# Packed attention scores, id transfers issued by ScalarE, and other part sizes in a graph-attention kernel

## The chip, the core and the metric

The kernel runs on one core of a Trainium2 chip. The core has five engines, each with its own instruction queue that it works through in order: PE (TensorE, matrix products into PSUM; PEld is its loading of stationary operands), DVE (VectorE), ACT (ScalarE), POOL (GpSimd) and SP (SyncE, which here only issues transfers). Transfers run on 16 DMA engines; SP, ACT and POOL can issue them. The metric is the device time of the kernel in microseconds.

## What is computed

One graph-attention layer with residual and two norms, over 12500 nodes and 412500 edges (D = 128, 64 edge features, 8 heads):

```python
h, q, k, v = (x @ W + b for each of Wn, Wq, Wk, Wv)
eh = edge_features @ We + be
hmid   = leaky_relu(concat(q[src], k[tgt], eh) @ A1 + b1, 0.2)
scores = leaky_relu(hmid @ A2 + b2, 0.2)            # 8 heads
w      = softmax(scores.mean(axis=-1), axis=0)      # over all edges
out    = segment_sum(w[:, None] * v[tgt], src)
y      = layernorm(h + out) * gamma + beta
return layernorm(x + y)
```

## The kernel before

Nodes lie in 98 blocks of 128, edges in 403 groups of 1024. The edges come in order of their target node; the sum goes by source node. So the kernel works in two halves.

**Making** (`make(p)`). For each group of a part p it builds one-hot matrices of the targets on DVE (lines 836 to 857), multiplies them on PE with the group's rows of the key and value table (line 914), adds the edge features' product (line 919), copies the result from PSUM to a record tile `rec` on ACT (lines 929 and 930), and POOL scatters the records by source block into a table in DRAM (line 941, eight scatters a group). Stage 0 makes part 0 alone, with the tables of the nodes and further index work spread between its groups.

**Summing** (`sums_of`). A part's table holds for each block a fixed number of tiles of 128 records, `plan.tiles[p]`, enough for the mean number of its edges and 4.4 standard deviations; unused places are masked. A unit is two blocks: 10, 12 or 14 tiles with 5, 6 or 7 tiles a block, 49 units a part. For each unit:

- SP loads the records `rt` (line 1109) and the blocks' query rows `qs`.
- `sources` makes the masked ids `sl` on DVE, `turn` transposes them on PE (line 1139), `turned` turns them into bytes `slT` on DVE (line 1146), `put` stores them in DRAM (`row`, line 1153) and `spread` loads them back, repeated over all partitions (`rowB`, line 1158). SP issues both transfers, and the second waits until the first has landed.
- For each piece of up to four tiles: one-hot `ohT` on DVE (line 1170), hidden layer on PE (lines 1184 and 1193), and its leaky rectifier in two steps, ACT (line 1204) and DVE (line 1208).
- `scores`: four products with `A2s` as the stationary operand, each over a fourth of the unit's tiles, into four strips of 32 PSUM partitions (line 1221). The 32 columns of `A2s` hold the eight heads and two columns of their sum, scaled, from which the linear part of the leaky rectifier comes. `above_zero` applies Relu with the bias on ACT (line 1235), and `heads` sums over heads: a product with `headsum` for each of three or four tile positions (line 1247).
- `maxima`, `maximum`, `reference` lower the running maximum over all partitions (lines 1257 to 1277), `weights` takes the exponential (line 1286), `select` and `weigh` make the weighted one-hots `ohw` (lines 1295 and 1309), and `add` sums the values by node (line 1338). `total` joins the partial sums of earlier parts (line 1354).

Stage p (1 to 5) interleaves the making of part p with the summing of part p - 1; then part 5 is summed alone, and the closing applies the softmax's sum and the norms. The parts are cut by `CUTS`, in groups; the last part ends at 403.

What sets the order: the engines' instructions stand in the order in which the program is written, with no reordering. A unit's operations are placed at steps by the offsets of `lags` and `last_lags` (eight steps from one unit to the next, six in the last part), and the steps are spread evenly over the six steps of each group being made. A line on an fp32 product stands for two passes on PE, so line 1221 has eight passes a unit. A record in the profile is one pass.

PSUM has eight banks: two for `pkv`, one for the counts, two for `ph`, one for `psc` (shared by the transposed ids and the scores) and two for `psm`.

## Time and profile before

| | us |
|---|---|
| median of three runs (4974.44 to 4991.73) | 4985.54 |
| the profiled execution | 4977.97 |
| its span | 4976.3 |

| engine | busy us | share of the span |
|---|---|---|
| PE | 4076.9 | 82% |
| PEld | 3176.9 | 64% |
| DVE | 4181.3 | 84% |
| ACT | 3168.0 | 64% |
| POOL | 3327.3 | 67% |

The granted clock of TensorE is 0.93 over the span, and the DMA engines move 294 GB/s. The busy shares are means over stages whose loads differ: making alone, making and summing together with different numbers of tiles a group, summing alone. They say little by themselves, so the span is best read in stretches, cut where a part ends (the mask of a part, line 978, is built once its last group is counted). Issuing a transfer and waiting for a semaphore are not counted as busy. An engine's wait is put down to whatever came last.

### The profile page before, as it was taken

The page shows a single profiled execution, that of the slowest core. Times are in us where ns is not written, and L with a number is a line of the kernel's source. Part 1 is how long each engine was busy: PE and PEld are TensorE (multiplying, and loading weights), DVE is VectorE, ACT ScalarE, POOL GpSimd, SP SyncE. Part 2 cuts the span into 40 slices and gives each one's busy share as a digit, 9 for nine tenths or more (in the row PEclk, how much of TensorE's full clock was granted, in tenths as well). Part 3 has the DMA queues.
Part 4 walks back from the last instruction along what each step waited for, and adds up shares of the span by engine and source line. Part 5 has one row for each costly group of instructions (what it writes and reads, how often), then busy time and mean ns, then how long its engine had stood idle before and what let it go on. Part 6 is the DMA issues. An engine that isn't in the chain of part 4 may idle for free. (4 is left out here: it accounts for less than half of the span.)

```text
span 4976.3 us, 87101 instructions
## 1 busy us (share of the span) xinstructions
PE 4076.9 (82%) x27267; PEld 3176.9 (64%) x27568; DVE 4181.3 (84%) x9010; ACT 3168.0 (64%) x8326; POOL 3327.3 (67%) x3280
## 2 busy tenths in 40 slices
PE   3665547878888989988988888988889888889997
PEld 2444435666666766776766676776667666666786
DVE  7888867888888888888988887888889898877777
ACT  2442224655656777777777776777777666667785
POOL 3777777777777777777777777767667777731003
PEclk7787868999999999999999999999999999999999
DMA  5888978999888998888898888888888898889864
GB/s 187 285 288 272 369 246 300 317 318 307 275 280 295 315 310 308 311 307 299 315 308 310 303 310 280 306 303 307 297 297 302 300 312 304 298 289 308 302 238 171
DMA packets 603263, 1462.23 MB, mean 294 GB/s; under 512 B 103678, under 2 KB 329105, under 8 KB 600996
## 3 DMA queue, kind: packets, MB, share of 16 engines
q1 hardware_dynamic: 447696, 1027.15, 62.9%
q0 software_dynamic: 154752, 429.39, 22.7%
q8 instruction: 220, 3.60, 0.3%
q14 instruction: 255, 2.09, 0.1%
q10 hardware_dynamic: 340, 0.01, 0.0%
HBM read 884.13 MB, written 585.06 MB: 295 GB/s over the span
## 5 line engine op out<-in xcount | busy, mean ns | idle before, releaser
L941 POOL DMA_INDIRECT rtab<-rec,idx x3224 | 3242.7, 1006 | 1150.6 <-issue 783.3
L929 ACT ACTIVATE rec<-pkv 128x1024 f32<-128x1024 f32 x806 | 821.6, 1019 | 1162.7 <-PE pkv L919 519.1
L1309 ACT ACTIVATE ohw<-ohs,w 128x128 f32<-128x128 bf16 x3822 | 1256.1, 399 | 121.8 <-DVE ohs L1295 59.0
L1338 PE MATMUL psm<-rt,ohw 128*128 128x128 f32 x7644 | 1085.4, 285 | 3.4 <-ACT ohw L1309 0.8
L1338 PEld LDWEIGHTS psm<-rt,ohw 128*128 128x128 f32 x7644 | 997.7, 197 | 101.4 <-ACT hm L1204 13.0
L919 PE MATMUL pkv<-WeS,eat 128*128 128x256 f32 x3224 | 920.5, 412 | 0.0
L1208 DVE TENSOR_TENSOR hm<-ph,hm 128x512 f32<-128x512 f32 (+1 forms) x1029 | 662.5, 644 | 265.9 <-ACT hm L1204 261.2
L914 PE MATMUL pkv<-kvs,ohd 128*128 128x256 bf16 x3224 | 530.0, 291 | 290.5 <-ACT rec L929 283.0
L1184 PE MATMUL ph<-ident,rt 128*128 128x128 f32 x3822 | 625.4, 284 | 118.1 <-DVE hm L1208 112.9
L1170 DVE TENSOR_SCALAR ohT<-rowB,iotaP,power 128x512 bf16<-128x512 uint8 (+2 forms) x1176 | 598.0, 519 | 93.0 <-DMA rowB<-row 92.7
L914 PEld LDWEIGHTS <-ohd 128*128 128x128 bf16 x3224 | 317.0, 103 | 540.6 <-issue 423.4
L919 PEld LDWEIGHTS pkv<-WeS,eat 128*128 128x128 f32 x3224 | 606.4, 209 | 70.2
L1184 PEld LDWEIGHTS ph<-ident,rt 128*128 128x128 f32 x3822 | 442.2, 146 | 323.9 <-issue 144.9
L1204 ACT ACTIVATE hm<-ph 128x512 f32<-128x512 f32 (+1 forms) x1029 | 567.0, 551 | 33.8 <-PE ph L1193 26.8
L857 DVE TENSOR_SCALAR ohd<-dstb,node 128x1152 bf16<-128x1152 uint8 x404 | 564.9, 1398 | 0.0
L1193 PE MATMUL ph<-ohT,qs 128*128 128x512 bf16 (+2 forms) x2051 | 531.6, 340 | 29.2 <-DVE ohT L1170 14.5
L883 DVE TENSOR_TENSOR ats<-pc,oh 128x792 f32<-128x792 f32 x403 | 391.1, 970 | 37.1 <-PE pc L865 37.1
L1221 PE MATMUL psc<-hm,A2s 128*32 128x384 f32 (+2 forms) x2352 | 360.0, 550 | 63.1 <-DVE hm L1208 34.4
L1295 DVE TENSOR_TENSOR ohs<-iotaE,sl 128x512 bf16<-128x512 bf16 (+1 forms) x1029 | 409.1, 398 | 1.0 <-ACT ohw L1309 1.0
L847 DVE TENSOR_REDUCE few<-oh 128x99 bf16<-128x792 bf16 x403 | 395.1, 980 | 13.9
L894 DVE TENSOR_REDUCE pos<-ats 128x8 f32<-128x792 f32 x403 | 389.1, 966 | 1.7
L1247 PE MATMUL psm<-headsum,z 128*128 128x4 f32 (+1 forms) x2058 | 256.7, 245 | 58.0 <-DVE part L1354 50.8
(192 smaller groups left out, 3876.2 us busy)
## 6 DMA issues: line engine op xcount, KB each, us to landing
rt<-rtab SPq DMA_DIRECT2D x147, 1820.0 KB
rt<-rtab SPq DMA_DIRECT2D x147, 1560.0 KB
eat<-in_ea SPq DMA_DIRECT2D x201, 512.0 KB
rtab<-rec,idx POOLq DMA_INDIRECT x3224
dstb<-dtab SPq DMA_DIRECT2D x201, 256.0 KB
rtab<-empty SPq DMA_DIRECT2D x76, 520.0 KB
qs<-qtab SPq DMA_DIRECT2D x294, 128.0 KB
atab<-part SPq DMA_DIRECT2D x294, 128.0 KB
```

Source lines behind the costliest of these rows:

```text
L857: nc.vector.tensor_scalar(to, ids[:, cols], node, None, op0=ALU.is_equal)
L914: nc.tensor.matmul(pk[:, i, h, :], ohd[t], kvs, start=(h == 0), stop=False,)
L919: nc.tensor.matmul(pk[:, i, :, :D], eat[:, (j + i) * P : (j + i + 1) * P], WeS, start=False, stop=True,)
L929: nc.scalar.activation(rec[:, :, :, : 2 * D], pk, AF.Copy)
L941: one_tile = nc.gpsimd.indirect_dma_start(out=rtab[p % TABS][:, :], out_offset=bass.IndirectOffsetOnAxis(ap=idxs[g][:, t : t + 1], axis=0) ...
L1170: nc.vector.tensor_scalar(st["oh"][k][:, (a - t0) * P : (b - t0) * P], st["rowB"][:, a * P : b * P], iotaP, power[:, bs[u] : bs[u] + 1], o ...
L1184: nc.tensor.matmul(ph[:, j * P : (j + 1) * P], st["rt"][:, t0 + j, :D], ident, is_transpose=True, start=(j == 0), stop=False,)
L1193: nc.tensor.matmul(ph[:, cols], st["qs"][:, j0 // t, s, :], oh[:, cols], start=False, stop=(s == 1 and j1 == t0 + n),)
L1204: nc.scalar.activation(hm, state[i]["ph", k][:, : n * P], AF.Copy, scale=SLOPE)
L1208: nc.vector.tensor_tensor(hm, ph[:, : n * P], hm, op=ALU.max)
L1309: nc.scalar.activation(ohw[:, j, :], ohs[:, :, j], AF.Copy, scale=st["w"][:, t0 + j : t0 + j + 1])
L1338: nc.tensor.matmul(st["psS"][:, (1 + u) * P : (2 + u) * P], ohw[:, j, :], st["rt"][:, t0 + j, D : 2 * D], start=(k == 0), stop=(k == t - 1),)
```

## The change

Four things change.

1. **Scores.** `A2s` becomes four operands of 32 columns; operand q holds the eight heads in columns 8q to 8q + 7 and zeros elsewhere. Tile t = 4q + s of a unit is multiplied with operand q into strip s of one 128x128 box, so that four tiles add up, side by side, in one strip. There is one product of 128 columns for each tile. The leaky rectifier is made exactly: ACT takes 0.2 (x + b2) of the box, and DVE (`peak`, a new step) the maximum of that and x + b2. `heads` is then a single product with `headsum`, one column a tile. `z` has 128 columns instead of 512 and two buffers instead of one.
2. **One bank.** `mix` holds two boxes for the scores, taken in turn, and a region of its own for the transposed ids.
3. **Ids.** `turned` moves from DVE to ACT, and ACT issues `put` and `spread` instead of SP.
4. **Parts.** Groups a part: 62, 73, 73, 73, 62, 60 before; 73, 73, 73, 73, 60, 51 now. Tiles a block: 6, 7, 7, 7, 6, 6 before; 7, 7, 7, 7, 6, 5 now. Both make 39 tiles a block, 3822 in all.

```diff
-CUTS = 0, 62, 135, 208, 281, 343
+CUTS = 0, 73, 146, 219, 292, 352
...
-    A2s = const.tile([D, 32], FP)
+    A2s = const.tile([D, 4, 32], FP)
...
+    for q in range(1, 4):
+        nc.vector.tensor_copy(A2s[:, q, q * H : (q + 1) * H], A2s[:, 0, :H])
+        nc.vector.tensor_copy(b2_r[:, q, :], b2_r[:, 0, :])
...
-    zp_ = pool("z", 1)
+    zp_ = pool("z", 2)
...
-    pscp = pool("psc", 1, space=PSUM)
+    mixp = pool("mix", 1, space=PSUM)
+    mix = mixp.tile([P, 4 * P], FP, name="mix")
...
-            st["pT"] = late.get("turn", pscp).tile([P, 4 * P], FP, name="psc")
+            st["pT"] = mix[:, 2 * P : 3 * P]
...
-            nc.vector.tensor_scalar(
-                st["slT"][:nt, :], st.pop("pT")[:nt, :P], 0.0, None, op0=ALU.max
-            )
+            nc.scalar.activation(st["slT"][:nt, :], st.pop("pT")[:nt, :P], AF.Relu)
...
-            nc.sync.dma_start(out=st["row"][:nt, :], in_=st.pop("slT")[:nt, :])
+            nc.scalar.dma_start(out=st["row"][:nt, :], in_=st.pop("slT")[:nt, :])
...
-            nc.sync.dma_start(
+            nc.scalar.dma_start(
                 out=st["rowB"][:, : nt * P],
...
+        def box(i):
+            return mix[:, i % 2 * P : (i % 2 + 1) * P]
+
+        def scores(i):
+            nt, hm = plans[i][0], state[i].pop("hm")[0]
+            for t in range(nt):
+                q, s = divmod(t, 4)
                 nc.tensor.matmul(
-                    psc[32 * q : 32 * q + 32, : n * P], A2s, hm[:, j * P : (j + n) * P],
-                    start=True, stop=True,
-                )
+                    box(i)[32 * s : 32 * s + 32, :], A2s[:, q, :], hm[:, t * P : (t + 1) * P],
+                    start=(q == 0), stop=(t + 4 >= nt),
+                )
...
+            nc.scalar.activation(
+                st["z"][:r, :], box(i)[:r, :], AF.Identity, bias=b2_c[:r, 1:2], scale=SLOPE
+            )
+
+        def peak(i):
+            st, r = state[i], 32 * min(4, plans[i][0])
+            nc.vector.scalar_tensor_tensor(
+                st["z"][:r, :], box(i)[:r, :], b2_c[:r, 0:1], st["z"][:r, :],
+                op0=ALU.add, op1=ALU.max,
+            )
...
+            nc.tensor.matmul(
+                st["psS"][:, :nt], st.pop("z")[:r, :], headsum[:r, :nt], start=True, stop=True
+            )
...
+            do(s0 + o["peak"], peak, i)
```

How the order moves, at three places. The line numbers after the change are about 10 to 18 lower.

PE at the scores of a unit of 14 tiles, near the end of stage 4; `mx` is the maximum, `rt` the records, `ohw` the weighted one-hots. Before:

```order
L1268 MATMUL psm<-ident,mx 128x128
L1338 MATMUL psm<-rt,ohw 128x128 x4
L1221 MATMUL psc<-hm,A2s 32x512 x3
L1221 MATMUL psc<-hm,A2s 32x256
L792 MATMUL pc<-firsts,ident 128x99
```

Now:

```order
L1250 MATMUL psm<-ident,mx 128x128
L1320 MATMUL psm<-rt,ohw 128x128 x4
L1208 MATMUL mix<-hm,A2s 32x128 x14
L784 MATMUL pc<-firsts,ident 128x99
L857 LDWEIGHTS above
```

Fourteen products of 128 columns stand where four of up to 512 stood; their neighbours are the same.

PE at the heads of the same unit, with the turning of a later unit's ids behind them. Before:

```order
L1338 MATMUL psm<-rt,ohw 128x128 x4
L1247 MATMUL psm<-headsum,z 128x4 x2
L1247 MATMUL psm<-headsum,z 128x3 x2
L1139 LDWEIGHTS sl
L1139 MATMUL psc<-identB,sl 14x128
```

Now:

```order
L1320 MATMUL psm<-rt,ohw 128x128 x4
L1231 MATMUL psm<-headsum,z 128x14
L1131 LDWEIGHTS sl
L1131 MATMUL mix<-identB,sl 14x128
L906 LDWEIGHTS ohd
```

One product takes the place of four.

ACT in stage 4 from the weighing of one unit to the weights of the next; `rec` is the evacuation of records that POOL scatters, `hm` the hidden layer's first step. Before:

```order
L1309 ACTIVATE ohw<-ohs,w 128x128 x4
L1204 ACTIVATE hm<-ph 128x384
L929 ACTIVATE rec<-pkv 128x4x256
L930 ACTIVATE rec<-srcl 128x4x4
L1309 ACTIVATE ohw<-ohs,w 128x128 x2
L1204 ACTIVATE hm<-ph 128x512
L929 ACTIVATE rec<-pkv 128x4x256
L930 ACTIVATE rec<-srcl 128x4x4
L1286 ACTIVATE w,sums<-S,ref 128x14
L1309 ACTIVATE ohw<-ohs,w 128x128 x4
L1235 ACTIVATE z<-psc,b_c 96x512
L1235 ACTIVATE z<-psc,b_c 32x256
```

Now:

```order
L1291 ACTIVATE ohw<-ohs,w 128x128 x4
L1138 ACTIVATE slT<-mix 14x128
L1143 DMA row<-slT 14x128
L1194 ACTIVATE hm<-ph 128x384
L921 ACTIVATE rec<-pkv 128x4x256
L922 ACTIVATE rec<-srcl 128x4x4
L1291 ACTIVATE ohw<-ohs,w 128x128 x2
L1194 ACTIVATE hm<-ph 128x512
L1148 DMA rowB<-row 128x1792
L1268 ACTIVATE w,sums<-S,ref 128x14
L1291 ACTIVATE ohw<-ohs,w 128x128 x4
L1216 ACTIVATE z<-mix,b_c 128x128
```

The bytes of the ids, their store and their spread stand on ACT, with one `hm`, one evacuation, two weighings and one more `hm` between store and spread; `z` is one instruction. The spread waits there for the store's landing. On SP's queue the two transfers are gone from between the loads of `kvs`, `qs`, `rt` and `old`.

98 lines of the change are left out of this document (29 added, 69 removed).

## Prediction

> **What bounds the kernel now.** I cut the span at the six instructions that build a part's mask (line 978 stands at each part's end: 714, 1476, 2237, 3000, 3733 and 4390 us) and read the busy time of each engine in the stretches between them. Stage 0 makes the records of part 0; stage p (1 to 5) makes part p and sums part p-1; the seventh stretch sums part 5; the last one is the closing. Columns: stretch, length, busy us (x instructions) of each engine, granted clock, DMA share, GB/s.
>
> ```profile
> 714.28 0.76 DVE L978 TENSOR_TENSOR mask<-placed,high 128x588 bf16<-128x588 f32 x1
> 3733.27 0.76 DVE L978 TENSOR_TENSOR mask<-placed,high 128x588 bf16<-128x588 f32 x1
> 0.00:714.00 714.00, 394.23 (x1517) 276.09 (x1518) 593.42 (x977) 227.22 (x312) 507.75 (x482) 0.77 0.83 281
> 714.00:1476.00 762.00, 592.17 (x3972) 456.46 (x4018) 611.98 (x1230) 429.07 (x1123) 582.13 (x589) 0.93 0.88 294
> 1476.00:2237.00 761.00, 672.62 (x4606) 529.02 (x4654) 667.40 (x1406) 543.66 (x1445) 582.16 (x588) 0.96 0.89 306
> 2237.00:3000.00 763.00, 673.98 (x4646) 530.05 (x4697) 671.42 (x1424) 554.17 (x1469) 584.70 (x586) 0.96 0.89 307
> 3000.00:3733.00 733.00, 646.98 (x4442) 508.12 (x4494) 617.48 (x1355) 530.00 (x1418) 506.30 (x509) 0.95 0.87 298
> 3733.00:4390.00 657.00, 579.40 (x4101) 455.26 (x4152) 580.63 (x1267) 456.85 (x1254) 477.22 (x483) 0.96 0.89 303
> 4390.00:4840.00 450.00, 416.13 (x3193) 325.32 (x3243) 339.95 (x960) 347.14 (x1079) 34.72 (x19) 0.99 0.82 280
> 4840.00:4976.00 136.00, 101.37 (x803) 96.56 (x803) 99.02 (x398) 79.89 (x231) 52.27 (x28) 0.91 0.51 191
> ```
>
> Stages 1, 2 and 3 make 73 groups each and last 762, 761 and 763 us, though stage 1 has 80 us less PE work. Something else paces them, and the timeline of POOL in the middle of stage 2 and its group there name it:
>
> ```profile
> 2003.11 0.96 POOL L941 DMA_INDIRECT rtab<-rec,idx  x1 [0.30 <-issue]
> L941 POOL DMA_INDIRECT rtab<-rec,idx x3224: 954/960/3228, 59.5 to 4395.4; - x190
> L941 POOL DMA_INDIRECT rtab<-rec,idx x588 | 583.4, 992 | 179.1 <-issue 144.1 <-ACT ohw L1309 7.9 <-DMA rtab<-rec,idx 7.3
> ```
>
> A scatter takes 0.96 us and the next starts 0.30 us later. Eight a group at 1.26 us are 10.1 us, 736 us for 73 groups of the 762 spent. POOL's busy share of 77% hides that it has no room: there, work taken off PE, DVE or ACT is worth nothing. In stages 4 and 5 a group takes 733/62 = 11.8 and 657/60 = 11.0 us, so POOL waits, and PE sets the pace: length over PE's busy time is 733/647 = 1.133 and 657/579 = 1.134, the same twice. In the summing stretch alone it is 450/416 = 1.08.
>
> **Parts of 73, 73, 73, 73, 60 and 51.** Tiles a block were 6, 7, 7, 7, 6, 6 and become 7, 7, 7, 7, 6, 5: 3822 in all both times, 49 units a part. So 11 groups move from stages 4 (2) and 5 (9) into stage 0, and 98 tiles from the summing stretch into stage 1. Stage 0 grows by 11 groups at the 10.4 us of stages 1 to 3 (762/73): +115. Its own mean, 714/62 = 11.5, gives +127; if the tables and edges, spread over more groups, no longer hold POOL, +83 (11 x 10.1, less the 28 us by which 714 exceeds a start of 59 and 62 x 10.1 us). I take +110. Stage 1 gets 14-tile units instead of 12, as stages 2 and 3 have; they show it costs nothing under POOL. So stages 1 to 3: 0, their cover being the scatters.
>
> **Heads.** The groups of stage 4 (busy, mean ns):
>
> ```profile
> L919 PE MATMUL pkv<-WeS,eat 128*128 128x256 f32 x496 | 133.8, 394 | 0.0
> L914 PE MATMUL pkv<-kvs,ohd 128*128 128x256 bf16 x496 | 79.0, 284 | 0.6 <-ACT rec L929 0.4
> L1221 PE MATMUL psc<-hm,A2s 128*32 128x512 f32 (+1 forms) x392 | 68.7, 592 | 12.3 <-DVE hm L1208 7.2 <-DVE slT L1146 5.1
> L1247 PE MATMUL psm<-headsum,z 128*128 128x4 f32 (+1 forms) x392 | 49.2, 249 | 17.5 <-DVE part L1354 14.9 <-ACT by L1328 1.7 <-ACT ohw L1309 0.9
> L1235 ACT ACTIVATE z<-psc,b_c 96x512 f32<-96x512 f32 x49 | 32.7, 668 | 0.5 <-PE psc L1221 0.5
> L1235 ACT ACTIVATE z<-psc,b_c 32x256 f32<-32x256 f32 x49 | 22.9, 466 | 0.6
> L1204 ACT ACTIVATE hm<-ph 128x512 f32<-128x512 f32 x98 | 56.9, 580 | 11.3 <-PE ph L1193 11.2
> L1204 ACT ACTIVATE hm<-ph 128x384 f32<-128x384 f32 x98 | 47.0, 480 | 2.2 <-PE ph L1193 1.1
> L1354 DVE SCALAR_TENSOR_TENSOR part<-old,by,psm 128x128 f32<-128x128 f32 x98 | 29.4, 340 | 6.1 <-PE psm L1338 5.6 <-PE pc L865 0.3
> L1146 DVE TENSOR_SCALAR slT<-psc 14x128 uint8<-14x128 f32 x49 | 13.4, 274 | 0.0
> L1309 ACT ACTIVATE ohw<-ohs,w 128x128 f32<-128x128 bf16 x682 | 225.1, 398 | 45.1 <-DVE S L1257 20.6 <-DVE ohs L1295 20.2 <-PE pkv L914 1.7
> ```
>
> Heads take 49.2/49 = 1.00 us a unit in eight passes; one product has two, 0.25 us. That is -0.75 us a unit of 14 tiles, and -0.5 with 12 (six passes).
>
> **Packed scores.** A unit's four score products, 384 or 512 columns each, become 10 to 14 of 128 columns, each with its own weights. Whether that costs PE depends on whether products into different 32-row strips still run side by side. The timeline of the summing stretch:
>
> ```profile
> 4601.86 0.16 PEld L1221 LDWEIGHTS psc<-hm,A2s 128*32 128x32 f32 x8
> 4601.86 0.85 PE L1221 MATMUL psc<-hm,A2s 128*32 128x384 f32 x8
> ...
> 4609.53 0.84 PE L1221 MATMUL psc<-hm,A2s 128*32 128x384 f32 x4
> ```
>
> Eight passes take 0.85 us and four take 0.84: strips overlap fully, two passes of 384 columns after one another in each. Packed, a strip holds three or four tiles of two 128-column passes, the same columns: 0 is my value. Bounds: -0.3 us a unit (only the last tiles now wait for the last hidden piece, where half did), and +2.6 if 28 passes at 0.13 us (0.85/768 x 128, less overlap) ran one by one, 3.7 against 1.1.
>
> In sentences the sum does without: the Trainium skill ("TensorE: Matmul & The Clock Gate", Part 3, The mechanism) says that a weight load overlaps running products only when the row group differs; all these products use all 128 rows, so by it each of up to 28 loads would stand alone. The eight loads above, done in 0.16 us beside the products, speak against it.
>
> **Rectifier and ids.** ScalarE's two passes over the scores (0.67 + 0.47 us; one of 0.56 with 12 tiles) become one of 128x128. From 512 and 384 columns at 0.58 and 0.48 us, 128 take about 0.28, at most the 0.40 of line 1309. DVE gains one product with maximum, 0.34 as line 1354, and loses slT, 0.27: +3 us a stage. The maximum stands one step behind ACT's pass on DVE and waits for it; queued behind it are the next one-hot, the hidden layer's maximum and then S, so a late pass would delay PE's next hidden piece as well. Before, the same step waited on PE instead, and the pass is 0.9 us shorter, so I add nothing. Scores no longer share their buffer with the turned ids (5.1 us of line 1221's idle in stage 4 ended with slT); that stays a bonus. The constants are prepared by about as many small instructions as before, on DVE ahead of the first scatter at 59 us: 0. ACT gains slT, about 0.28. It also issues two transfers; their price on ACT is bounded by the issues that it makes at the start and by SP's own:
>
> ```profile
> rt<-rtab SPq DMA_DIRECT2D x147, 1820.0 KB
> 6.24 1.76 ACTq L528 DMA_DIRECT2D b_c<-b_d  x4
> L1153 SPq DMA_DIRECT2D row<-slT x294: 315/362/794, 765.3 to 4810.9; - x147
> SPq L1158 <- DMA row<-slT: 199.1, 45, 8.9
> SPq L1158 <- DMA row<-slT: 186.0, 51, 7.7
> SPq L1158 <- DMA row<-slT: 31.5, 23, 3.6
> DVE ohT L1170 <- DMA rowB<-row: 33.8, 20, 5.5
> DVE sl L1131 <- DMA rt<-rtab: 30.8, 16, 5.8
> ```
>
> 0.32 to 0.44 us each; 0.36 taken. With 0.2 for the store's wait for slT (an estimate, half an activation) ACT gains per unit -0.86 + 0.28 + 0.72 + 0.2 = +0.3 us with 14 tiles and, from -0.28 instead of -0.86, +0.9 with 12. In stage 4 that makes 545 us of ACT: hidden beside PE's 600.
>
> Of the five last rows the first is from stage 4, the next two from stage 5 and the summing stretch, the rest from stage 4: SP stands 199.1/45 = 4.4 us after each store until the ids have landed, with rt, qs, eat and kvs loads queued behind it, and DVE waits 34 us for rowB and 31 for rt. On ACT the same wait would hold the weights, the evacuation of records and so POOL. But between store and spread ACT now has hm, rec, two weighings and hm, about 3.0 us, and the store no longer queues behind SP's rt loads of 1.8 MB; the shortest mean wait (31.5/23 = 1.4 us) is where SP has no record loads. I take 0 hold there; bounds 0 and 4.4 - 3.0 = 1.4 us a unit.
>
> **The sum.** Stage 4: PE 647 less 37 for heads and 2 groups at 3.4 us (133.8 + 79.0 over 62): 603; times 1.133 is 683. POOL's 60 groups need 606 and DVE's 617 hardly falls, so three engines close up, and I take 688: -45 (bounds -90, where they overlap as in stage 3, and 0). Stage 5: PE 579 less 25 and 9 x 3.4 = 523, times 1.134 is 593; DVE, as long as PE before (581), loses the nine groups but no heads, so I take 600: -57 (-90 to -25). Summing stretch: its rows are
>
> ```profile
> L1338 PE MATMUL psm<-rt,ohw 128*128 128x128 f32 x1297 | 178.3, 280 | 3.2 <-ACT ohw L1309 0.8
> L1184 PE MATMUL ph<-ident,rt 128*128 128x128 f32 x627 | 97.1, 278 | 0.0
> L1193 PE MATMUL ph<-ohT,qs 128*128 128x256 bf16 (+1 forms) x366 | 82.7, 319 | 5.3 <-DVE ohT L1170 4.5 <-issue 0.2
> L1309 ACT ACTIVATE ohw<-ohs,w 128x128 f32<-128x128 bf16 x650 | 213.0, 400 | 7.8 <-DVE S L1257 5.8
> ```
>
> A tile costs PE (178.3 + 97.1 + 82.7)/650 = 0.55 us. Two fewer and the heads are -1.6 us a unit, PE 416 - 78 = 338. ACT saves 2 x 0.33 on weighing and 0.2 on hm and pays 0.9: 347 stays about the same and becomes the bound. 347 x 1.08 = 375 would be -75; with PE and ACT this close I take -50 (bounds -80 and -15). In all +110 - 45 - 57 - 50 = -42 us. The profiled execution took 4978 us (span 4976), 7.6 under the median 4985.5; on the median's footing 4943.
>
> **Rivals.** First: the stages in which PE leads gain little, since DVE, POOL and ACT are as near; stages 4, 5 and the summing stretch give -20, -45 and -40: with +110 that is +5, 4990, no change. For it: the three totals near 606 in stage 4. Against: stage 3 fills 763 us with PE at 674 and POOL full, so close totals can overlap. Second, the slower one: ACT stands at the spread until the ids have landed. With the hold of 1.4 us in stage 4 and 0.6 in stage 5 (186.0/51 = 3.6, less 3.0), 49 units each, +69 and +29 on my sum: 5041. It decides from 0.43 us of hold a unit in both stages (42 us over 98 units). The Trainium skill ("DMA: Bandwidth & Descriptors", Issuing engines are not separate DMA queues) speaks for it: transfers of all issuers run on the same engines, and another issuer saves only issue time; then the ids land no sooner, and it is this rival. No row of before has an id transfer on ACT to show it. Third: the strips do not overlap when weights change at each product. At +2.6 us stages 4, 5 and the sum lose 144, 144 and about 60, and stages 1 to 3 turn PE-bound, (640 + 127) x 1.133 = 869 each, 107 more: 144 + 144 + 60 + 321 = 669 on my sum, 5612. Against it stand the eight passes in 0.85 us. Fourth, the move frees nothing, because rowB and rt were late for the transfers' own length: the sum stays, since it counts none of those 65 us.
>
> **Chances.** My forecast 0.58, with its own range 4875 to 4970; the first rival 0.20; ACT held 0.13; strips in turn 0.06; a gain beyond my bounds (stages 4 and 5 at POOL's floor, 606 and 515) 0.03; the fourth lies in the forecast. Within 0.3%, about what a measurement of this kernel can tell from no change, are 4971 to 5000. Of the first rival half lies there and a quarter on either side. Faster 0.58 + 0.03 + 0.05 = 0.66; same 0.10; slower 0.13 + 0.06 + 0.05 = 0.24. The range, 4865 to 5041, takes in the first two rivals and leaves out the third, half of the beyond and the upper part of the second.
>
> **What would show it.** Right: stage 0 near 825 us, stages 1 to 3 at 762 with POOL's gap at 0.30; line 1208 near 1.1 us a unit on PE; the spread's wait on ACT's queue well under 0.5 us a unit; stages 4 and 5 under 700 and 610. Wrong: products of line 1208 that start 0.1 us apart over 3 us, ACT idle before hm or rec behind line 1148, or stage 0 over 840.

## The result

The changed kernel takes 4987.8 us (median of 19 runs, 4962.5 to 4992.6), the kernel before 4978.7 us in 19 runs taken with them (4966.7 to 4991.7). The ratio is 1.0013, 95% interval 1.0002 to 1.0024: some 0.1% slower, which the prediction's bound of 0.3% counts as no change. Forecast was 4943 us, a gain of 42 us. The profiled execution (span 4987.7 us, granted clock 0.923) in the stretches used before, cut at the parts' masks; columns as there (stretch, length, busy us of PE, PEld, DVE, ACT, POOL, granted clock, DMA share, GB/s):

```profile
0.00:827.00 827.00, 454.78 (x1715) 315.22 (x1716) 644.34 (x1037) 251.91 (x356) 593.52 (x573) 0.73 0.81 271
827.00:1593.00 766.00, 606.39 (x4961) 497.64 (x5007) 643.99 (x1313) 469.66 (x1305) 583.41 (x593) 0.93 0.85 294
1593.00:2351.00 758.00, 636.11 (x5330) 525.44 (x5379) 672.75 (x1417) 516.39 (x1462) 579.07 (x584) 0.97 0.90 309
2351.00:3106.00 755.00, 637.73 (x5335) 526.50 (x5385) 675.14 (x1426) 519.70 (x1469) 577.02 (x585) 0.97 0.91 310
3106.00:3798.00 692.00, 594.71 (x5089) 497.16 (x5140) 611.96 (x1340) 488.08 (x1408) 489.15 (x496) 0.96 0.91 313
3798.00:4431.00 633.00, 531.54 (x4546) 430.88 (x4591) 543.79 (x1216) 432.46 (x1264) 404.08 (x409) 0.98 0.87 293
4431.00:4851.00 420.00, 362.77 (x3333) 298.31 (x3381) 312.37 (x956) 307.67 (x1027) 32.87 (x17) 0.98 0.79 263
4851.00:4988.00 137.00, 101.51 (x802) 96.58 (x801) 100.17 (x402) 80.80 (x235) 52.28 (x28) 0.92 0.51 191
```

| stretch | before | after | difference | forecast |
|---|---|---|---|---|
| stage 0 | 714 | 827 | +113 | +110 |
| stages 1, 2, 3 | 762, 761, 763 | 766, 758, 755 | -7 | 0 |
| stage 4 | 733 | 692 | -41 | -45 |
| stage 5 | 657 | 633 | -24 | -57 |
| summing part 5 | 450 | 420 | -30 | -50 |
| closing | 136 | 137 | +1 | 0 |
| sum | 4976 | 4988 | +12 | -42 |

All rows but two came out to within 7 us. Stage 5 and the summing stretch were 33 and 20 us short, and that is nearly the whole miss of 54 us. (Stage 4 came out near its forecast for other reasons than the forecast's; see below.) In stage 5 PE's busy time fell nearly as reckoned (579 to 532 us, 523 forecast), but the stretch did not follow: length over PE's busy time was 1.13 before and is 633/532 = 1.19 now. What the other forecasts of the profile were worth, in three views: POOL's timeline in stage 2; the groups of the scores, of the heads' products in units of 14 tiles and of all the heads' weight loads, over the whole run; and the waits of ACT in the summing stretch.

```profile
1980.46 0.96 POOL L933 DMA_INDIRECT rtab<-rec,idx  x1 [0.30 <-issue]
L1208 PE MATMUL mix<-hm,A2s 128*32 128x128 f32 x7644 | 313.0, 280 | 62.0 <-DVE hm L1198 60.6 <-ACT slT L1138 0.7 <-issue 0.2
L1231 PE MATMUL psm<-headsum,z 128*128 128x14 f32 x392 | 67.8, 248 | 55.6 <-DVE z L1222 54.0
L1231 PEld LDWEIGHTS psm<-headsum,z 128*128 128x128 f32 x588 | 89.6, 192 | 112.5 <-DVE z L1222 98.5 <-PE psm L1320 7.3 <-issue 5.4
ACT w L1268 <- DVE ref L1259: 35.9, 49, 4.9
ACT hm L1194 <- DMA row<-slT: 23.6, 17, 2.6
```

The scatters keep their gap of 0.30 us. The 26 passes of packed scores of a mean unit take 313.0/294 = 1.06 us, where 26 one after another at the prediction's 0.13 us would take 3.4: the strips run side by side. But the heads' loads now wait 98.5 us over the run for `z` from VectorE's maximum, and their products 54.0 us in units of 14 tiles, a wait for which the sum added nothing. In the summing stretch ACT stands 23.6 us behind the ids' landing.

### The profile page after: what moved, and what is told of

The parts are those of the page before. It is cut to its first block, busy times and chain, and to the rows that moved or that the text cites. A ratio compares the mean times of both kernels' runs of the same rounds, so it can differ in the third digit from the quotient of the medians.

```text
span 4987.7 us, 95043 instructions
## 1 busy us (share of the span) xinstructions
PE 3925.6 (79%) x31094; PEld 3187.7 (64%) x31390; DVE 4204.5 (84%) x9101; ACT 3066.7 (61%) x8522; POOL 3311.4 (66%) x3282
## 3 DMA queue, kind: packets, MB, share of 16 engines
q8 instruction: 249, 4.08, 0.3%
## 5 line engine op out<-in xcount | busy, mean ns | idle before, releaser
L1320 PE MATMUL psm<-rt,ohw 128*128 128x128 f32 x7644 | 1100.1, 285 | 30.9 <-ACT ohw L1291 30.6
L1320 PEld LDWEIGHTS psm<-rt,ohw 128*128 128x128 f32 x7644 | 1010.6, 196 | 136.1 <-ACT ohw L1291 41.5
L1198 DVE TENSOR_TENSOR hm<-ph,hm 128x512 f32<-128x512 f32 (+2 forms) x1078 | 669.8, 621 | 143.4 <-ACT hm L1194 141.5
L1160 DVE TENSOR_SCALAR ohT<-rowB,iotaP,power 128x512 bf16<-128x512 uint8 (+3 forms) x1176 | 590.6, 509 | 127.0 <-DMA rowB<-row 126.5
L1194 ACT ACTIVATE hm<-ph 128x512 f32<-128x512 f32 (+2 forms) x1078 | 578.1, 536 | 161.6 <-ACT slT L1138 34.5
L1183 PE MATMUL ph<-ohT,qs 128*128 128x384 bf16 (+3 forms) x2056 | 538.9, 340 | 36.9 <-DVE ohT L1160 22.9
L1277 DVE TENSOR_TENSOR ohs<-iotaE,sl 128x512 bf16<-128x512 bf16 (+1 forms) x1078 | 424.9, 394 | 1.1 <-ACT ohw L1291 1.1
L1208 PE MATMUL mix<-hm,A2s 128*32 128x128 f32 x7644 | 313.0, 280 | 62.0 <-DVE hm L1198 60.6
L1268 ACT ACTIVATE w<-S,ref 128x14 f32<-128x14 f32 (+2 forms) x294 | 88.9, 303 | 338.0 <-DVE ref L1259 208.6
```

What stands on the lines that cost most here:

```text
L1160: nc.vector.tensor_scalar(st["oh"][k][:, (a - t0) * P : (b - t0) * P], st["rowB"][:, a * P : b * P], iotaP, power[:, bs[u] : bs[u] + 1], o ...
L1183: nc.tensor.matmul(ph[:, cols], st["qs"][:, j0 // t, s, :], oh[:, cols], start=False, stop=(s == 1 and j1 == t0 + n),)
L1194: nc.scalar.activation(hm, state[i]["ph", k][:, : n * P], AF.Copy, scale=SLOPE)
L1198: nc.vector.tensor_tensor(hm, ph[:, : n * P], hm, op=ALU.max)
L1320: nc.tensor.matmul(st["psS"][:, (1 + u) * P : (2 + u) * P], ohw[:, j, :], st["rt"][:, t0 + j, D : 2 * D], start=(k == 0), stop=(k == t - 1),)
```

## The experiments

The kernels ran on two kinds of chips. On some the kernel before takes 4979 to 4987 us, as in the result (4980 chips below). On others, with the same program, it takes 5832 to 5903 us (5830 chips). Every ratio is to the kernel before on the same chip. Below, "packing" is the new scores with their rectifier and heads (points 1 and 2 of the change), "ids" is point 3, and "the last stretch" is the summing of part 5 and the closing together (557 us in the changed kernel, 586 before). The theories: A, the gain is eaten by the heads' wait for VectorE's maximum; B, the new parts cost more than the +110 and what stages 4 and 5 give back; C, the ids' transfers cost ACT time; D, a guess added when the first four runs had landed on a 5830 chip: there TensorE is supplied slowly with instructions, and packing has more of them.

### One part of the change alone, and one part undone

The parts alone, on the kernel before (twice: `c_only` on a 5830 chip, `c_only_2` on a 4980 chip):

```diff
-CUTS = 0, 62, 135, 208, 281, 343
+CUTS = 0, 73, 146, 219, 292, 352
```

> The kernel before with the new parts alone (73, 73, 73, 73, 60, 51). Theory A (the gain of packing is eaten by the wait of the heads for the new maximum on DVE): the parts alone are about even, since 11 groups cost stage 0 some 113 us and give back 11 x 3.9 us in stages 4 and 5 and 98 tiles x 0.6 us in the summing stretch: 0 to +15 us. Theory B (the parts cost more than I counted and eat the gain): +30 us or more, stages 4 and 5 near the lengths they had before less 10 and 30 us.

> The kernel before with the parts of 73, 73, 73, 73, 60 and 51 groups alone. Where the kernel before takes 4980 us: if the parts are neutral as on the other chips, 0.998 to 1.003, stage 0 at 827, stages 4 and 5 at 710 and 632. If the parts carry all of the gain of stages 4 and 5 (TensorE paces neither), stage 5 is 632 as in the changed kernel; if TensorE paces it (my forecast), some 25 us longer, 655.

Measured: 5830 chip 1.0011 (0.9995 to 1.0026), 4980 chip 1.0103 (1.0085 to 1.0121), some 51 us slower.

Without packing: the same cuts and, on the kernel before, the ids on ScalarE (`i_c` on a 5830 chip, `i_c_2` on a 4980 chip):

```diff
-            nc.vector.tensor_scalar(
-                st["slT"][:nt, :], st.pop("pT")[:nt, :P], 0.0, None, op0=ALU.max
-            )
+            nc.scalar.activation(st["slT"][:nt, :], st.pop("pT")[:nt, :P], AF.Relu)
...
-            nc.sync.dma_start(out=st["row"][:nt, :], in_=st.pop("slT")[:nt, :])
+            nc.scalar.dma_start(out=st["row"][:nt, :], in_=st.pop("slT")[:nt, :])
...
-            nc.sync.dma_start(
+            nc.scalar.dma_start(
```

> The changed kernel without packing: the parts of 73, 73, 73, 73, 60 and 51 groups, and the ids turned by ScalarE and moved from its queue, with scores, rectifier and heads as before. C (the ids' transfers cost ScalarE): 1.005 to 1.010 of the kernel before. D (the loss is packing's): 0.998 to 1.003, and few stretches of one product each 0.72 us. Where the kernel before takes 4980 us, A (packing's waits eat the gain of the heads): about 1.000, no better than the changed kernel by more than 0.3%.

> The changed kernel without packing. Where the kernel before takes 4980 us: if TensorE's work does not pace stages 4 and 5, these are 692 and 632 as in the changed kernel and the last stretch is 20 us longer than its 557, 1.000 to 1.006 of the kernel before; if it does (my forecast), stages 4 and 5 are 20 to 40 us longer each, 1.010 to 1.018. If packing costs there what it costs on the other chips, 0.988 to 0.992.

Measured: 5830 chip 1.0047 (1.0031 to 1.0064), 4980 chip 1.0127 (1.0110 to 1.0144). The stretches of stage 4, stage 5 and the last one with the closing on a 4980 chip, of parts alone and then of parts and ids:

```profile
3115.00:3829.00 714.00, 635.54 (x4401) 504.66 (x4454) 608.69 (x1341) 527.75 (x1410) 492.34 (x494) 0.96 0.88 302
3829.00:4464.00 635.00, 558.73 (x3950) 437.98 (x3999) 540.21 (x1216) 440.96 (x1226) 415.11 (x413) 0.96 0.86 292
4464.00:5032.00 568.00, 489.96 (x3692) 398.77 (x3740) 412.60 (x1356) 411.98 (x1252) 84.86 (x45) 0.97 0.71 242
```

```profile
3110.00:3821.00 711.00, 631.35 (x4403) 496.48 (x4456) 601.11 (x1293) 533.94 (x1458) 490.54 (x494) 0.98 0.89 304
3821.00:4449.00 628.00, 550.30 (x3926) 426.67 (x3974) 530.43 (x1164) 444.62 (x1265) 409.01 (x411) 0.99 0.88 295
4449.00:5027.00 578.00, 493.74 (x3712) 401.07 (x3761) 398.34 (x1305) 424.16 (x1314) 85.84 (x46) 0.96 0.70 237
```

On 4980 chips the result is thus a sum of two terms of opposite sign. The parts cost 1.0%; ids on ScalarE add 0.2% (not told from zero: the two intervals overlap), and packing, from 1.0127 to 1.0013, gives 1.1%, some 57 us. (The last ratio is from another 4980 chip than the first two; its interval, 1.0002 to 1.0024, lies clear of theirs.) Theory B holds there. Stage 5 is 635 us with the parts alone, 628 with parts and ids and 633 with all three, where the expectation had 655 for the parts alone if PE paced it: the parts alone made that stage what it is, and packing gave it nothing that these profiles show. Packing gives in stage 4 (711 to 692) and at the end (578 to 557). The profiled execution of parts and ids was 20 us shorter than that kernel's median, so its stretches may be up to that much too short in all, and the gains of packing by stage too small.

The changed kernel with the old parts (`p_i`) and with the ids back on VectorE and SP (`p_c`), both on a 5830 chip; their edits are the two diffs above in the other direction:

> The changed kernel with the old parts (62, 73, 73, 73, 62, 60): packing and ids alone. Theory A: little, -25 to 0 us, with PE's heads still waiting for z about 170 us in all. Theory B: -30 to -60 us, the gain that the parts then eat. Theory C (the ids' transfers on ACT cost): +0 to +20 us.

> The changed kernel with the ids' rectifier on DVE and both transfers on SP again. Theory A: within 10 us of the changed kernel. Theory C (rowB comes later from ACT's queue: DVE waits 126 us for it against 93 before, 42 against 0.4 in stage 5): 20 to 40 us faster than the changed kernel, rowB waits back near 90 us in all.

Measured: 1.0150 (1.0122 to 1.0177) and 1.0133 (1.0104 to 1.0161), so theory B's gain without the parts did not show (`p_i` is some 88 us slower than the kernel before), nor the 20 to 40 us that theory C had for `p_c`: `heads_late` on the same chip as `p_c`, with the ids on ScalarE and the heads one step later, has 1.0145. The changed kernel itself on another 5830 chip, and the kernel before once more for its stretches, as bases:

> The changed kernel itself, as the base for the kernels run beside it (on the chip of the earlier runs every packed kernel took 1.3 to 1.5% more than the kernel before, on the first chip the changed kernel took 0.1% more). A and C (waits in the changed order): the same loss whatever the chip, 1.000 to 1.003. D (ten more TensorE instructions a unit, which that chip supplies slowly): about 1.001 on a chip where the kernel before takes 4980 us, 1.013 to 1.016 where it takes 5830 us, with stages 1 to 3 some 10 us longer each there.

> The kernel before, for its stretches on a chip where it takes 5830 to 5900 us. All theories: its last stretch (summing part 5 and the closing) 580 to 590 us as on the first chip (586), since no record is scattered there; stages 1 to 3 near 935 to 950 (the parts-only kernel's 930 to 948). The doubled heads' 601 in that last stretch then is +15 for 37 us of TensorE.

Measured: 1.0179 (1.0156 to 1.0202) for the changed kernel; the kernel before landed on a 4980 chip (4983 us), not on a 5830 chip as expected, so no stage of the runs on 5830 chips has a base in the kernel before. Its stretches are as in its first profile but for stage 5, 668 us in place of 657, so that one profile tells a stage to some 10 us. On 5830 chips the parts are neutral (1.0011), and packing, which gives 1.1% on 4980 chips, costs over 1% (from 1.0011 with the parts alone to 1.0133 when packing is added, on the same chip).

### The heads' wait for the maximum

Heads one step later (`heads_late` and, beside the changed kernel, `heads_late_2`; both on a 5830 chip):

```diff
-            leaky=2, scores=L + 1, above=L + 2 + e, peak=L + 3 + e, heads=L + 3 + 2 * e, maxima=f, maximum=f + 1,
+            leaky=2, scores=L + 1, above=L + 2 + e, peak=L + 3 + e, heads=L + 4 + 2 * e, maxima=f, maximum=f + 1,
...
-            peak=L + 4, heads=L + 5, maxima=f, maximum=f + 1, reference=f + 2 + e, weights=f + 3 + e,
+            peak=L + 4, heads=L + 6 if e else L + 5, maxima=f, maximum=f + 1, reference=f + 2 + e, weights=f + 3 + e,
```

> The changed kernel with the heads' product one step later in units of 13 or 14 tiles and in all parts but the last (in the last part only units of over 12 tiles, so there is no change there); the maxima stay where they were. Theory A: PE's wait for z falls from 172 us to under 60 in all, stages 4 and 5 fall by 15 to 30 us each, the total by 30 to 60 us. Theories B and C: within 10 us of the changed kernel.

> The changed kernel with the heads one step later in the order (the other stages of the softmax where they were). A: 0.985 to 0.99 of the changed kernel. Rival (the heads' place is not what holds it; S and the maximum come as late as before): within 0.4% of the changed kernel, with VectorE's wait for psm in place of TensorE's wait for z.

ScalarE's pass and the maximum one step earlier (`peak_early`, a 5830 chip), and the maximum left out (`no_peak`, a 5830 chip):

```diff
-            leaky=2, scores=L + 1, above=L + 2 + e, peak=L + 3 + e, heads=L + 3 + 2 * e, maxima=f, maximum=f + 1,
+            leaky=2, scores=L + 1, above=L + 1 + e, peak=L + 2 + e, heads=L + 3 + 2 * e, maxima=f, maximum=f + 1,
...
-            spread=-turn + 5, q=-9, onehot=-2, sloped=1, leaky=2, scores=L + 1, above=L + 3,
-            peak=L + 4, heads=L + 5, maxima=f, maximum=f + 1, reference=f + 2 + e, weights=f + 3 + e,
+            spread=-turn + 5, q=-9, onehot=-2, sloped=1, leaky=2, scores=L + 1, above=L + 2,
+            peak=L + 3, heads=L + 5, maxima=f, maximum=f + 1, reference=f + 2 + e, weights=f + 3 + e,
```

```diff
-            do(s0 + o["peak"], peak, i)
```

> The changed kernel with ScalarE's pass over the scores and VectorE's maximum one step earlier, the heads where they were, so that a step lies between maximum and heads. A: as without the product, stages 4, 5 and the sum shorter by 60 to 90 us together, ratio to the changed kernel 0.982 to 0.99. Rival: ScalarE now meets the scores earlier than TensorE has made them and waits for TensorE instead, with its two leaky passes behind; within 0.4% of the changed kernel or up to 1% slower.

> The changed kernel without VectorE's product with maximum: z holds only 0.2 times the scores plus bias, so the positive branch of the rectifier is left out and the output differs. The heads then wait for ScalarE's pass alone. A (the gain is eaten by the heads' wait for that product): stages 4 and 5 and the summing stretch lose most of the 32, 37 and 24 us that TensorE stood at the heads, 4915 to 4940 us where the changed kernel takes 4988, 0.985 to 0.99 of it. Rival (that wait is only where TensorE happens to stand; ScalarE's weighing and VectorE's one-hots set the pace): the wait moves to the maximum or to the sums, within 0.4% of the changed kernel. D: the same as the rival on every stage.

Measured on the same chip, where the changed kernel has 1.0179: heads later 1.0184 (1.0161 to 1.0207), pass and maximum earlier 1.0323 (1.0305 to 1.0340, worse than either theory had it; the cause was not looked for), without the maximum 1.0197 (1.0170 to 1.0225). (The first run of heads later: 1.0145, 1.0120 to 1.0171, on the chip where `p_c` had 1.0133.) Taking the waited-for operation away gives nothing. On a 4980 chip the same was tried in the kernel with one-pass scores and the ids on SP (next part), where the waits for `z` are longer (172.0 us of the loads): 1.0046 without the maximum, 1.0052 with it, and stage 4, stage 5 and the last stretch 709, 632 and 543 us against 712, 634 and 544, where theory A had 10 us or more in each. Theory A falls on both kinds: PE's wait for `z` is where it happens to stand.

### What TensorE's time is worth

Each product of the heads twice, on the kernel before (`heads_twice`, a 5830 chip); one-pass scores on the changed kernel (`scores_bf16`, a 5830 chip), and with the ids back on VectorE and SP (`bf16_sp`, a 4980 chip; `bf16_sp_nopeak` also without the maximum); the packed products issued strip by strip (`strip_major`, a 4980 chip):

```diff
-            for j in range(sw):
+            for j in [*range(sw), *range(sw)]:
```

```diff
+    A2h = const.tile([D, 4, 32], BF)
+    nc.vector.tensor_copy(A2h, A2s)
...
-                st["hm"][t0 - c] = hp.tile([D, TM * P], FP, name="hm")
+                st["hm"][t0 - c] = hp.tile([D, TM * P], BF, name="hm")
...
-                    box(i)[32 * s : 32 * s + 32, :], A2s[:, q, :], hm[:, t * P : (t + 1) * P],
+                    box(i)[32 * s : 32 * s + 32, :], A2h[:, q, :], hm[:, t * P : (t + 1) * P],
```

```diff
-            for t in range(nt):
+            for t in sorted(range(nt), key=lambda t: t % 4):
```

> The kernel before, with every product of the heads issued twice (the second overwrites the first with the same values): 2058 more products and 2058 more weight loads, 1.0 us more of TensorE in a unit of 14 tiles and 0.75 in one of 12. It measures what TensorE time of the heads is worth. TensorE sets the pace (my forecast): stages 4 and 5 and the summing stretch +55, +42 and +40 us. Rival (waits set the pace there, and TensorE's time is taken out of them): under half of that, under 70 us in the three together. D (TensorE is supplied slowly with instructions on chips where the kernel before takes 5830 to 5900 us): there also +10 to +20 us in each of stages 1 to 3, and twice the stretches in which TensorE starts a product every 0.72 us (40 with 117 us in the parts-only kernel), 1.008 to 1.012 in all; where the kernel before takes 4980 us, none of these.

> The changed kernel with the hidden layer's maximum and the attention weights in bfloat16, so that a score product is one pass and not two: 14 products and 14 loads less in a unit of 14 tiles, about what packing added and more. The scores lose precision. D: on chips where the kernel before takes 5830 to 5900 us the whole loss of 1.3 to 1.8% goes, to 0.995 to 1.005 of the kernel before, and the stretches of one product each 0.72 us fall from about 100 to 50. A and C (waits for the maximum and for the ids): the loss stays, 1.012 to 1.018, since only 0.5 us of TensorE a unit is saved. Where the kernel before takes 4980 us: D says no more than 0.5% better than the changed kernel.

> The changed kernel with one-pass scores (hidden maximum and attention weights in bfloat16, scores less precise) and with the ids turned by VectorE and moved from SP's queue, as before. C (the ids on ScalarE cost 0.3 to 0.4%, 11 us of it in the last stretch): 0.990 to 0.993 of the kernel before, last stretch 523 to 528 us against 537 of one-pass scores alone. Rival (their price belongs to the two-pass scores' own delays): as one-pass scores alone, 0.995 to 0.997, last stretch 535 to 538.

> The kernel of one-pass scores with the ids on SP, without VectorE's maximum: z holds only 0.2 times the scores plus bias, so the positive branch of the rectifier is left out and the output differs. A (the heads' wait for the maximum takes the gain): stages 4 and 5 and the last stretch 10 us or more shorter each than with it, 0.993 of it or less. Rival: the last stretch about 10 us shorter, the rest as with it, 0.997 to 1.000.

> The changed kernel with a unit's score products issued strip by strip (all tiles of the first 32 rows, then of the next) and not tile by tile, the same number of instructions. Side by side only when neighbours in the order go to different strips: the 28 passes then take 3 to 3.7 us of TensorE a unit in place of 1.06 and 1.5, the last stretch grows by 40 to 90 us, 1.04 to 1.08 of the kernel before on a chip where it takes 5830 to 5900. If the hardware still overlaps them: as the changed kernel. If it is the 28 in a row without waiting that starve TensorE of instructions, the stretches of one product each 0.72 us fall from about 100 to 50.

Measured: heads twice 1.0184 (1.0165 to 1.0204, more than theory D had), one-pass scores 0.9956 (0.9939 to 0.9972) on one and the same 5830 chip. On a 4980 chip: one-pass scores with ids on SP 1.0052 (1.0037 to 1.0068), without the maximum 1.0046 (1.0028 to 1.0064), strip by strip 1.0061 (1.0039 to 1.0082). Stage 4, stage 5 and the last stretch on a 4980 chip, strip by strip and then one-pass scores with the ids on SP, and the group of the scores strip by strip:

```profile
3110.00:3801.00 691.00, 628.95 (x5089) 537.25 (x5136) 613.57 (x1342) 486.95 (x1408) 485.22 (x493) 0.98 0.92 313
3801.00:4437.00 636.00, 563.27 (x4529) 467.63 (x4578) 542.71 (x1212) 432.35 (x1262) 406.99 (x411) 0.98 0.87 291
4437.00:5014.00 577.00, 486.97 (x4141) 419.45 (x4189) 416.53 (x1360) 391.37 (x1262) 85.23 (x46) 0.96 0.71 238
L1208 PE MATMUL mix<-hm,A2s 128*32 128x128 f32 x7644 | 573.5, 281 | 56.7 <-DVE hm L1198 55.8 <-ACT slT L1138 0.7
```

```profile
3119.00:3831.00 712.00, 581.80 (x4411) 482.94 (x4461) 620.88 (x1391) 480.31 (x1359) 493.87 (x495) 0.94 0.88 303
3831.00:4465.00 634.00, 525.19 (x3935) 427.41 (x3984) 552.12 (x1263) 426.96 (x1221) 412.10 (x410) 0.94 0.86 292
4465.00:5009.00 544.00, 448.45 (x3597) 388.56 (x3645) 428.54 (x1409) 373.56 (x1204) 86.77 (x46) 0.93 0.74 253
```

Strip by strip the scores take 573.5/294 = 1.95 us of PE a unit, and stages 4 and 5 are 691 and 636 us: 34 and 32 us more of PE time than in the changed kernel cost 0 and 3 us. Stage 5 was 628 to 636 us in six kernels of these parts whose PE work there went from 515 to 563 us. PE does not set its pace. In the last stretch PE's time does count: strip by strip +23 us of it gave +20, and one-pass scores alone, with 14 us less, have 537 us (on a 5830 chip, where the changed kernel has 557 too). The doubled heads, with 34 us more of PE than the kernel before, have 601 us against 586: +15, under half of the +40 expected if PE set the pace. The ids' price there is not one number. With ids on ScalarE the last stretch is 10 us longer on a 4980 chip and 14 on a 5830 chip without packing (568 to 578, 563 to 577), 14 on a 5830 chip with packing (545 in `p_c`, 559 in `heads_late`), but one-pass scores with the ids on SP have 544 us, not the 523 to 528 that theory C had, and no less than the 537 with the ids on ScalarE. Stage 4 is shortest, 691 to 692 us, only where packing and ids on ScalarE come together; with one alone it is 711 or 712, with neither 714. (The kernel that stands here for packing alone has one-pass scores. With two-pass scores there is a pair on one 5830 chip: 829 us with ids on SP in `p_c`, 811 with ids on ScalarE in `heads_late`, whose heads stand one step later.)

The waits of SP in stage 4 show what the ids' move does there, first of the parts alone, then of the changed kernel:

```profile
SPq L1158 <- DMA row<-slT: 195.6, 47, 8.3
SPq L1153 <- DVE ohT L1170: 109.5, 23, 7.8
SPq L1153 <- DVE slT L1146: 95.7, 25, 5.6
```

```profile
SPq L1101 <- PE psm L1320: 156.9, 32, 13.9
SPq L1101 <- PE pc L857: 48.4, 8, 9.8
SPq L800 <- PE psm L1320: 42.4, 13, 10.2
```

SP stood 401 us at the ids' store and spread; now it stands mostly at its loads of records (line 1101), which wait for PE to free a buffer: it runs ahead. The Trainium skill ("DMA: Bandwidth & Descriptors", Issuing engines are not separate DMA queues) says that issuing from several engines saves only the time of issuing. The traces show something besides: SP's queue also held the 401 us of waits, and the move takes them away. That these waits are what the move saves is not shown: with parts and ids alone SP waits for its buffers likewise (170.3 us at the records), and stage 4 is 3 us shorter (714 to 711); with packing the move goes with 20 us (712 to 692).

### The moved bytes

In stage 4 the changed kernel moves 313 GB/s with 0.91 of the DMA engines busy, the most of any stretch. To see whether that sets its length, every unit's `qs` is loaded a second time into a tile that nothing reads (`qs_twice`, a 4980 chip):

```diff
+    morep = pool("more", 2)
...
+            more = morep.tile([P, 2, 2, D], HF, name="more")
+            nc.sync.dma_start(
+                out=more[:, : len(bs), :, :].rearrange("p b s d -> p b (s d)"),
+                in_=qtab[:, bs[0] : bs[-1] + 1, :],
+            )
```

> The changed kernel with every unit's qs loaded a second time, into a tile that nothing reads: 6.4 MB more a part, 3% of what stages 2 to 4 move at 309 to 313 GB/s. If the transfers' throughput paces stage 4, it grows from 692 by some 20 us, and stages 2 and 3 (309 and 310 GB/s) by 15 to 20 too: 1.010 to 1.015 of the kernel before. If the scatters' 1.26 us pace stages 1 to 3 (my forecast) and the order's waits stage 4, nothing grows by more than 5 us: 1.000 to 1.004.

```profile
1604.00:2368.00 764.00, 641.26 (x5340) 528.99 (x5389) 673.93 (x1419) 516.82 (x1463) 581.77 (x585) 0.96 0.92 315
3126.00:3819.00 693.00, 596.88 (x5103) 497.63 (x5153) 613.30 (x1344) 488.48 (x1410) 494.73 (x495) 0.97 0.93 322
4460.00:5036.00 576.00, 477.33 (x4142) 407.28 (x4190) 414.94 (x1358) 391.18 (x1262) 85.65 (x46) 0.94 0.73 249
```

Measured 1.0086 (1.0061 to 1.0111), between the two expectations, but not where throughput would have put it: stage 4 is 693 us at 322 GB/s (+1) and stage 2 764 (+6). The rest is 19 us at the end, 12 in stage 0 and 8 in stage 5, against "nothing grows by more than 5 us"; its cause was not looked for.

## Why the prediction was wrong

**Stage 0 and the scatters.** +110 forecast, +113 measured, +117 with the parts alone; stages 1 to 3 stood at 755 to 768 us on 4980 chips while PE's work in them went from 583 to 676 us. Right, and right for the reason given: the gap between scatters stayed at 0.30 us.

**Packed scores and heads.** The value 0 for the scores held at 1.06 us a unit, and the third rival fell, even strip by strip (1.95 us, not 3.7). Packing was worth 57 us on 4980 chips. By the forecast's own terms the heads were worth (37 + 25) x 1.13 in stages 4 and 5 and 0.5 x 49 = 25 x 1.08 in the summing stretch, some 97 us. The profiles show 19 us of it in stage 4, 21 at the end and none in stage 5.

**Stage 4, right by luck.** -45 forecast, -41 measured, but by other shares: the forecast had -42 for the heads (37 x 1.133), -8 for the two groups and +5 for engines that close up; measured were -19 for the parts alone (733 to 714), -3 when the ids moved and -19 when packing came. The heads' term was twice too large here as well, and the two groups made up for it.

**Stage 5, the step that failed.** "PE 579 less 25 and 9 x 3.4 = 523, times 1.134 is 593 [...] I take 600". PE came to 532 and the stage to 633. The step took the ratio of length to PE's busy time, the same 1.13 in two stages, as a proof that PE sets the pace. It was a coincidence: with the parts alone the ratio is 635/559 = 1.14, changed 1.19, strip by strip 1.13, all at the same length. So the 28 us put on the heads there (25 x 1.134) came to nothing. What paces the stage in PE's place is not shown. ACT's wait for the lowered maximum is long in stage 5 of before, of the changed kernel and strip by strip:

```profile
ACT w L1286 <- DVE ref L1277: 87.6, 39, 4.3
```

```profile
ACT w L1268 <- DVE ref L1259: 108.1, 42, 5.6
```

```profile
ACT w L1268 <- DVE ref L1259: 105.3, 39, 5.2
```

But a wait is not yet the path. Followed back from the stage's end, each instruction to what released it by the times of the semaphores, the path through these three stages has 15, 24 and 22 us in the softmax's steps from heads to weights, and 107, 46 and 83 us in PE's products. The largest share is transfers under way: 215, 242 and 210 us, in the kernel before mostly scatters (142) and loads of records (69), in the other two mostly the ids' spread `rowB` (146 and 117). The same shows in DVE's wait for `rowB` in stage 5, before and changed:

```profile
DVE ohT L1170 <- DMA rowB<-row: 0.4, 1, 0.4
```

```profile
DVE ohT L1160 <- DMA rowB<-row: 42.3, 23, 4.1
```

With one-pass scores and the ids on SP that wait is 3.7 us, DVE waits 32.8 us for records instead, and the stage is 634 us all the same: one wait takes the other's place. No run shortened both, so what paces stage 5 stays open. The parts' own term was nearly right: the nine groups moved out of stage 5 gave 22 to 33 us there (635 against 657 and 668), which the forecast had at 9 x 3.4 x 1.134 = 35.

**The summing stretch, the second miss.** -50 forecast, -30 measured: -18 with the parts alone (450 to 432), +10 for the ids, -22 for packing. Two parts of that step failed. "A tile costs PE (178.3 + 97.1 + 82.7)/650 = 0.55 us. Two fewer and the heads are -1.6 us a unit": that is a mean, not what a tile less saves. It makes 54 us of PE for the 98 tiles; with the parts alone PE came down 29 (416 to 387), and in the changed kernel to 363, not 338. Rows of the changed kernel in that stretch, against 178.3, 97.1 and 82.7 us before:

```profile
L1320 PE MATMUL psm<-rt,ohw 128*128 128x128 f32 x1101 | 170.8, 296 | 3.2 <-ACT ohw L1291 3.0
L1174 PE MATMUL ph<-ident,rt 128*128 128x128 f32 x526 | 86.9, 281 | 0.0
L1183 PE MATMUL ph<-ohT,qs 128*128 128x384 bf16 x98 | 24.7, 334 | 0.0
L1183 PE MATMUL ph<-ohT,qs 128*128 128x512 bf16 x60 | 22.4, 387 | 7.6 <-DVE ohT L1160 6.9 <-issue 0.2 <-DMA atab<-part 0.2
L1183 PE MATMUL ph<-ohT,qs 128*128 128x256 bf16 x110 | 21.3, 281 | 0.0
L1183 PE MATMUL ph<-ohT,qs 128*128 128x128 bf16 x98 | 13.8, 223 | 0.0
```

15% fewer passes of `psm` take 4% less time (0.155 us a pass in place of 0.137), and the query products stay at 366 recorded passes and 82.2 us, because a unit of ten tiles is cut into as many pieces as one of twelve. And "I take 0 hold there" for the ids was low in that stretch: ids on ScalarE made it 10 to 14 us longer in three pairs of kernels (above), 0.2 to 0.3 us a unit, inside the bound of 1.4 but not 0. In stages 4 and 5, where the second rival was priced at 69 and 29 us, ACT's waits behind the ids' transfers come to 16 us at most and to none: there the rival fell.

**The maximum.** "Before, the same step waited on PE instead, and the pass is 0.9 us shorter, so I add nothing": PE's loads wait 98.5 us for `z`, yet the runs without the maximum gained nothing. The value was right; the row of the wait would have misled.

**The rivals.** The first, that stages 4, 5 and the sum give -20, -45 and -40 for a total of +5, has nearly the right total (+12 measured) and fits the kind of miss, engines close together without one bound; its split is wrong. By parts of the change the runs on 4980 chips give: parts +51 us (the forecast's own terms give 110 - 8 - 35 and, for 54 of the 78 us of PE in the sum, -35: +32), ids about +12 with an interval that holds 0, packing -57.

**What stays open.** Packing and ids with the old parts would be the best candidate on 4980 chips, by the ratios 1.0013/1.0103 = 0.991, an estimate that takes the terms to add up; it ran only on a 5830 chip, at 1.0150. No kernel here was shown to beat the kernel before on a 4980 chip; on a 5830 chip one-pass scores did (0.9956), at the price of less precise scores.

## What to carry to other kernels

Length over the busy time of the busiest engine is no proof of a bound, even when two stages agree: vary that engine's work in the stage (double it, or halve it) before pricing a saving by the ratio. Do not price a removed tile by the mean of its lines: the passes that stay can take longer. And split a change of several parts before trusting its total: here a gain of 1.1% and a loss of 1.0% made a flat result.

## What the runs showed of the hardware

Two kinds of chips run this program 17 to 19% apart, and a change can have opposite signs on them. On 5830 chips PE takes instructions in places at one product each 0.72 us or its double, with no wait that the profile shows. The timeline of PE in stage 2 of the changed kernel on a 5830 chip, and its group of the scores over the run:

```profile
2302.49 0.27 PE L1320 MATMUL psm<-rt,ohw 128*128 128x128 f32 x1 [0.84 <-issue]
2303.95 0.27 PE L1320 MATMUL psm<-rt,ohw 128*128 128x128 f32 x1 [1.18 <-issue]
2304.67 0.27 PE L1320 MATMUL psm<-rt,ohw 128*128 128x128 f32 x1 [0.46 <-issue]
2305.39 0.35 PE L1320 MATMUL psm<-rt,ohw 128*128 128x128 f32 x1 [0.45 <-issue]
2305.67 1.49 PE L1208 MATMUL mix<-hm,A2s 128*32 128x128 f32 x28
```

```profile
L1208 PE MATMUL mix<-hm,A2s 128*32 128x128 f32 x7644 | 438.5, 298 | 246.6 <-issue 220.8 <-DVE hm L1198 20.2 <-ACT slT L1138 2.1
```

On 4980 chips the idle time before that group that ended with issue is 0.2 us, here 220.8. Counting stretches of over 2 us in which the products start 0.62 to 0.82 us or twice that apart, the traces have at most two on 4980 chips, 41 (119 us) with the parts alone on a 5830 chip, 102 (355 us) with the changed kernel, 44 (117 us) with the heads twice and 59 (178 us) with one-pass scores. So they do not follow the number of instructions alone, as theory D had it (for the heads twice it expected twice 40). The time does not follow it in proportion either. Each pass has one weight load: 27666 with the parts alone, 31390 changed, 27568 with one-pass scores, at ratios of 1.0011, 1.0179 and 0.9956, so that 3700 to 3800 passes go with 1.7 to 2.2%, though PE's busy time was lower with more of them (4417 us changed, 4487 with the parts alone); the heads twice have 2058 more than the kernel before and 1.8%. These ratios are from three 5830 chips. The last stretch, in which nothing is scattered, shows none of the difference (557 us for the changed kernel on either kind). What makes those chips slow in supplying PE, the runs don't tell. The Trainium skill ("Runtime: NRT & Kernel Launch", Instruction fetch mechanics) says that fetching instructions is mostly hidden; the traces agree as far as they show it. The packets of the larger instruction queue (249 of them, 4.08 MB) take 1.06 us each in the mean on a 4980 chip and 1.08 on a 5830 chip, and the slow stretches begin anywhere between two of them, so that fetching is not shown to be the cause of the 220.8 us.
